# Side work that states how long it holds PSUM, and begins a chain only where the chain fits

## The chip, the cores and the metric

The kernel runs on one core of a Trainium2 chip. The core has a matrix engine (TensorE, PE in the profile; its weight loads are PEld), a vector engine (VectorE, DVE), an activation engine (ScalarE, ACT), a general engine (GpSimd, POOL) and an engine that here only issues DMAs (SyncE, SP). Each engine works through its own queue in order; semaphores make one wait for another. The metric is the device time of one launch in microseconds, lower is better.

## The reference

The input is an image batch of 4 x 64 x 64 pixels with 96 channels. Four layers follow each other, each with a residual sum. Layers 0 and 1 are selective scans over the image; layers 2 and 3 are an attention of linear form and a feed-forward net with values quantized to 8 bits. Cut to the scan layers, whose side work is what changes:

```python
x = x + conv_ref(_gn(x), ...)                  # layers 0 and 1
    xz = x @ in_proj_w.T;  xi, z = split(xz)   # 96 -> 192 + 192
    xc = silu(depthwise_conv3x3(xi) + conv_b)
    xs = four orders of the pixels of xc       # K = 4 directions
    dts, Bs, Cs = split(einsum(xs, x_proj_w))  # per pixel: 6 + 16 + 16
    delta = softplus(dts @ dt_w + dt_b);  A = -exp(A_logs)
    h = exp(delta * A) * h + delta * u * B     # along 4096 pixels, 16 states
    y = sum over states of h * C  + D * xs;  back to image order, summed over K
    y = (y - mean) * rsqrt(var + 1e-5) * ln_w + ln_b
    out = (y * silu(z)) @ out_proj_w.T         # 192 -> 96
t = t + attention(ln(t));  t = t + ffn(ln(t))  # layers 2 and 3
```

`_gn` normalizes groups of three channels over the whole image, so a layer's convolution can begin only when its input's statistics are there.

## The kernel before, in words

**Phases, blocks, tiles.** A phase is one scan layer for one pair of images: phases 0 and 1 are layer 0, phases 2 and 3 layer 1. Two images share the 128 partitions. A phase has 16 blocks (4 directions k by 4 stretches t of 1024 pixels), and a block 48 tiles: 2 groups g of 8 states, 3 channel groups j, 8 states n. A tile is one state's scan over 1024 pixels for 64 channels of two images, 3,072 tiles in all. The main loop (L1046) goes through them by number i; i modulo 48 is called the tile's place in its block.

**What a tile does.** `begin` (two tiles ahead) makes the decay exp(delta A) on ACT in a buffer f, or, for five of 16 states (`POOL_N`), the product with B on POOL, and then the decay goes to the PSUM buffer psB (`decays`). `row` spreads B into psB with PE for the others, `product` multiplies it on DVE. `scan` (L684, DVE) runs the recurrence, `weigh` (L695, POOL) multiplies by C, `gather` sums pairs of tiles into psY with PE. B and C rows come by DMA as copies `brep` and `crep` (L642) on SP's queue, seven to nine tiles ahead.

**The next block's preparation.** `prepare` puts the tasks for the next block (loads, permutation, projections, softplus, copies) at fixed places of the current one. It uses the two PSUM slots called psM, and returns `kept`, the 16 places 17 to 32 (before a block with k = 0) or 13 to 28 (before others), in which psM belongs to it.

**Side work.** Two generators give all other work of the scan layers in pieces; each `yield` ends a piece. `behind(ph)` sets their order: in phase 0 the rest of its own convolution and that of phase 1; in phase ph the tail of phase ph-1, then the convolution of phase ph+1; in phase 3 also the weights of the feed-forward net and the first 12 units of its own tail.

- `conv_pieces`: statistics of the input (16 loads, `bn_stats`, two small matmuls with a psM slot each), then 8 tiles of 512 pixels. A tile has 3 chains j: 9 taps of two matmuls each into the slot px (L289), Silu to xo (L296), two matmuls into the slot pz (L299), Silu to zo (L304), and two stores (L305, L306). `load` fetches the padded input of the next tile. `done` counts finished tiles.
- `tail_pieces`: 16 units of 256 pixels per phase: load yu and zu, transpose into two psM slots (L360) with statistics on ACT, a power on POOL (L372), normalize, transpose back into psM (L387), scale on ACT (L392), gate by z on DVE (L398), the last projection into psM plus the residual xr (L426 to L442), copies and stores. `ready` counts finished units.

**The driver.** In each step of the main loop outside `kept`, `advance` takes one piece (L1090). What a piece yields tells whether it left a psM slot in use: `True` or `MORE` for yes, `False` for no; `MORE` marks a convolution tap, of which a second is taken in the same step when the convolution is behind its goal (`late_by`). Before `kept` begins, the slots must be free, so at its first place all pieces up to the next `False` are taken in one step (L1085 to L1087). Two other loops take pieces without a bound: at place `min(nexts)` until the next block's convolution tiles are finished (L1081 to L1084), and at a phase's change until all are (L1071).

**The last stage.** After the tiles, layers 2 and 3 are put in order by `run`, which keeps a model time for each of its threads. One thread, `remaining`, takes one tail piece at a time; quarters of images 2 and 3 wait for the tail's units. DMAs of all stages are issued by SP in the order of the program.

Of the kernel before, what the change touches and what calls it, by code (L numbers as in the profile page):

```python
# [15 lines left out]
C = 96  # L16
# [18 lines left out]
def kernel(ctx: ExitStack, tc: tile.TileContext, ins, out, layers=(0, 1, 2, 3)):  # L35
# [131 lines left out]
    def mlp_weights():  # L167
# [11 lines left out]
        def quantized(q, src, shape):  # L179
            t = wide(shape, "wq")  # L180
            nc.sync.dma_start(t, src)
            yield False
            yield False
            nc.vector.tensor_copy(q, t, saturate=False)
# [22 lines left out]
    MORE = 2  # L207
# [4 lines left out]
    def conv_pieces(w, xin, xc, zg, done):  # L212
# [9 lines left out]
        yield False  # L222
        yield False
        for i in range(2):
            stats = small([C, NT, 6], "gst")
            for t in range(NT):
                if t:
                    yield False
# [5 lines left out]
            yield False  # L234
            pm = psM([C, 1])
            nc.tensor.matmul(pm, gmat, mv[:, 0:1], start=True, stop=True)
            yield True
# [6 lines left out]
            yield False  # L244
            pv = psM([C, 1])
            nc.tensor.matmul(pv, gmat, dev, start=True, stop=True)
            yield True
# [4 lines left out]
            yield False  # L252
# [23 lines left out]

        done.append(now[0])
        coming = load(0)
        for t in range(NT):
            pads, coming = coming, None  # L280
            yield False
            for i in range(2):
                nc.scalar.activation(pads[i][1], pads[i][1], AF.Identity, bias=norms[i][1], scale=norms[i][0])  # L283
            yield False
            for j in range(J):
                px = psM([128, T])
                for tap in range(9):
# [6 lines left out]
                    yield MORE if tap < 8 else True  # L294
# [3 lines left out]
                for i in range(2):  # L298
# [3 lines left out]
                    )  # L302
                zo = thin([128, T], "zo")
                nc.scalar.activation(zo, pz, AF.Silu)  # L304
                nc.sync.dma_start(xc[:, j, t * T : (t + 1) * T], xo)  # L305
                nc.sync.dma_start(zg[:, j, t * T : (t + 1) * T], zo)  # L306
                if j == J - 1 and t + 1 < NT:
                    coming = load(t + 1)
                if j == J - 1:
                    done[0] += 1  # L310
                yield False

    def tail_pieces(w, units, y, zg, xin, xout, tokens):
# [10 lines left out]
        coming = None  # L324
        for t in units:
            tt = slice(t * U, (t + 1) * U)
            if coming is None:
                while t * U >= flushed(y):
                    yield False
                coming = load(t)  # L330
                yield False
                yield False
# [4 lines left out]
            xr = st([C, 2, U], F32, "xr", 1)  # L337
            for i in range(2):
                nc.sync.dma_start(xr[:, i, :], xin[i][:, tt])
# [17 lines left out]
            for q in range(2):  # L357
# [5 lines left out]
                if q:  # L363
                    statistics(0, pts)
                pts = pt
                yield True
            statistics(1, pts)
            yield False
# [5 lines left out]
            yield False  # L374
            yield False
# [25 lines left out]
            yield False  # L401
            pn0 = back(0)
            normalize(1)
            yield True
            scaled(pn0)
            pn1 = back(1)
            yield True
            scaled(pn1)
            yield True
            gate(0, pn0)  # L410
# [3 lines left out]
            yield True  # L414
            gate(1, pn1)
            yield True
            if tokens:
                xo = thin([128, 2, 2, C], "xn")
                pos = []
                for i in range(2):  # L420
# [8 lines left out]
                    yield True  # L429
                for i in range(2):  # L430
                    nc.scalar.copy(xo[:, i], pos[i][:, :, 0:C])
                    nc.sync.dma_start(xout[i][tt].rearrange("(q p) c -> p q c", p=128), xo[:, i])
                ready[0] = t + 1
            else:
                xo = thin([C, 2, U], "xn")
                pos = []
                for i in range(2):
# [5 lines left out]
                    yield True  # L443
# [768 lines left out]
```

## Time and profile before

| | us |
|---|---|
| median of three runs (11153.49 to 11181.56) | 11167.48 |
| the profiled execution's own time | 11149.85 |
| its span, from the first to the last instruction | 11148.1 |
| first scan L684 starts, last one ends | 134.5, 10545.7 |
| mean granted PE clock | 0.87 |

The profile is of one execution. Busy time of an engine is the sum of its instructions; idle time is given with the instruction that it came before and what ended it, so "<-DVE f L684 296.6" in a row of POOL reads: before such instructions POOL sat idle and a scan on DVE ended 296.6 us of that. A row of the form `L695 POOL TENSOR_TENSOR f<-f,crep 128x1024 f32 ... x3072 | 7158.9, 2354 | ...` gives line, engine, operation, tiles, shape, number, busy time and mean duration in ns. The busy share in 40 equal slices shows where the engines are dense:

```profile
PE   7978888777777779887788878887778877778777
DVE  3898999999999889989999999999999999999846
ACT  3656556554566646665566656665466655555576
POOL 3989999999999889999999999999999999999846
PEclk8989999888888889998888889998888888888877
```

A digit is tenths of a slice of 279 us. POOL and DVE are nearly full from the second slice to the 37th, PE and ACT are not. The first slice and the last two are outside the tiles or nearly.

### The profile page before, as it was taken

How to read it: one execution, taken by the hardware profiler on the slowest of the kernel's cores; microseconds unless marked ns; L12 is line 12 of the kernel's file. 1: busy time of each engine (PE TensorE's matmuls, PEld its weight loads, DVE VectorE, ACT ScalarE, POOL GpSimd, SP SyncE). 2: the span in 40 equal slices, each digit the busy share in tenths (PEclk: the TensorE clock that was granted, in tenths of full speed). 3: DMA queues.
4: the chain of work that ended last, by engine and by line, in shares of the span. 5: the costliest groups of instructions: out<-in, count | busy, mean ns of one | idle time of the engine just before them, and what ended most of it. 6: DMA issues, size and time to landing. Idle time of an engine off the chain costs nothing. (4 is left out here: it accounts for less than half of the span.)

```text
span 11148.1 us, 101994 instructions
## 1 busy us (share of the span) xinstructions
PE 8910.0 (80%) x30112; PEld 2880.5 (26%) x30112; DVE 9926.4 (89%) x6431; ACT 6423.1 (58%) x10575; POOL 10204.6 (92%) x5102
## 2 busy tenths in 40 slices
PE   7978888777777779887788878887778877778777
PEld 2222222111222212221222222222222322222365
DVE  3898999999999889989999999999999999999846
ACT  3656556554566646665566656665466655555576
POOL 3989999999999889999999999999999999999846
PEclk8989999888888889998888889998888888888877
DMA  5679976897578885798666656665556565556410
GB/s 134 158 141 162 141 160 157 145 134 136 149 171 151 140 151 149 157 159 132 138 169 157 157 146 169 164 159 143 149 157 156 155 149 148 143 137 159 122 33 22
DMA packets 1848188, 1604.57 MB, mean 144 GB/s; under 512 B 1412298, under 2 KB 1482892, under 8 KB 1847628
## 3 DMA queue, kind: packets, MB, share of 16 engines
q1 hardware_dynamic: 1847628, 1598.04, 66.1%
q8 instruction: 237, 3.88, 0.2%
q14 instruction: 323, 2.65, 0.1%
HBM read 1008.37 MB, written 186.65 MB: 107 GB/s over the span
## 5 line engine op out<-in xcount | busy, mean ns | idle before, releaser
L695 POOL TENSOR_TENSOR f<-f,crep 128x1024 f32<-128x1024 f32 x3072 | 7158.9, 2354 | 395.9 <-DVE f L684 296.6
L727 PE MATMUL psY<-f,fold 128*64 128x512 f32 x12288 | 3795.1, 698 | 183.4 <-POOL f L695 182.8
L684 DVE TENSOR_TENSOR_SCAN f<-f,state,psB 128x1024 f32<-128x1024 f32 x1584 | 3717.8, 2347 | 206.2 <-ACT f L669 50.1
L669 ACT ACTIVATE f<-delta,L_a 128x1024 f32<-128x1024 f32 x2112 | 2406.5, 1145 | 903.9 <-PE psY L727 829.8
L676 DVE TENSOR_TENSOR psB<-psB,du 128x1024 f32<-128x1024 f32 x2112 | 2558.9, 1212 | 362.9 <-PE psB L662 322.1
L662 PE MATMUL psB<-spB,sel 96*128 96x512 bf16 x4224 | 1387.8, 414 | 1613.5 <-DVE f L684 1599.0
L652 POOL TENSOR_TENSOR f<-du,brep 128x1024 f32<-128x1024 f32 x960 | 2265.7, 2360 | 127.2 <-PE psY L727 29.4
L684 DVE TENSOR_TENSOR_SCAN f<-psB,state,f 128x1024 f32<-128x1024 f32 x720 | 1676.7, 2329 | 76.8 <-POOL f L652 50.3
L727 PEld LDWEIGHTS psY<-f,fold 128*64 128x64 f32 x12288 | 974.9, 154 | 2525.3 <-issue 1806.8
L690 ACT COPY state<-f 128x1 f32<-128x1 f32 x2304 | 429.7, 188 | 2065.8 <-DVE f L684 2056.7
L669 ACT ACTIVATE psB<-delta,L_a 128x1024 f32<-128x1024 f32 x960 | 1070.2, 1115 | 696.0 <-DVE f L684 636.1
L684 DVE TENSOR_TENSOR_SCAN f<-f,psB 128x1024 f32<-128x1024 f32 x528 | 1208.3, 2288 | 57.6 <-ACT f L669 5.9
L662 PEld LDWEIGHTS <-sel 96*128 96x128 bf16 x4224 | 271.3, 99 | 3320.4 <-DVE f L684 2163.7
L289 PE MATMUL psM<-pad,wf 96*64 96x512 f32 x3456 | 901.4, 623 | 36.0 <-ACT pad L283 28.9
L684 DVE TENSOR_TENSOR_SCAN f<-psB,f 128x1024 f32<-128x1024 f32 x240 | 545.6, 2273 | 102.9 <-ACT psB L669 60.0
L718 PE MATMUL psY<-ysum,ident 128*128 128x512 f32 x768 | 554.5, 862 | 98.3 <-ACT ynew L743 86.7
L585 POOL TENSOR_TENSOR xs<-delta,xs 128x1024 f32<-128x1024 f32 x192 | 452.7, 2358 | 95.0 <-ACT delta L582 95.0
L569 PE MATMUL psM<-proj,dtw 12*128 12x512 f32 x768 | 455.2, 686 | 0.0
L543 PE MATMUL psM<-xs,xp 128*76 128x512 f32 x768 | 414.7, 651 | 5.5 <-DMA xs<-xcd 4.2
L718 PE MATMUL psY<-yold,ident 128*128 128x512 f32 (+2 forms) x960 | 370.6, 526 | 42.2 <-ACT ysum L739 26.7
L289 PEld LDWEIGHTS psM<-pad,wf 96*64 96x64 f32 x3456 | 221.4, 138 | 501.0 <-issue 422.6
L743 ACT COPY ynew<-psY 128x1024 f32<-128x1024 f32 (+2 forms) x312 | 242.4, 818 | 171.5 <-PE psY L727 171.5
(149 smaller groups left out, 6644.6 us busy)
## 6 DMA issues: line engine op xcount, KB each, us to landing
crep<-bc SPq DMA_DIRECT2D x2048, 256.0 KB, 4.8
delta<-delta SPq DMA_DIRECT2D x768, 256.0 KB, 4.8
du<-xs SPq DMA_DIRECT2D x768, 256.0 KB, 6.2
brep<-bc SPq DMA_DIRECT2D x640, 256.0 KB, 4.9
yd<-ynew SPq DMA_DIRECT2D x192, 512.0 KB, 7.8
xraw<-xcd SPq DMA_DIRECT2D x144, 512.0 KB, 8.5
yold<-yd SPq DMA_DIRECT2D x144, 512.0 KB, 8.9
xcd<-xo SPq DMA_DIRECT2D x96, 256.0 KB, 3.0
```

The lines of the kernel that those rows point to most:

```text
L289: nc.tensor.matmul(px[64 * i : 64 * i + 64], w["wf"][:, tap, 64 * j : 64 * j + 64], pads[i][0][:, tap // 3 : tap // 3 + rows, tap % 3 : ta ...
L569: nc.tensor.matmul(pds[-1], order[0][1][64:76, j, :], rests[s][64:76], start=True, stop=True)
L585: nc.gpsimd.tensor_mul(xs[j], deltas[j], xs[j])
L652: nc.gpsimd.tensor_mul(f[:, 1:], made[at]["dus"][j][n % 2], reps[at, 0, n])
L662: nc.tensor.matmul(scanned[i][0][:, ss], sel[:, n, :], made[at]["parts"][:, ss], start=True, stop=True)
L669: nc.scalar.activation(out, made[at]["deltas"][j][n % 2], AF.Exp, scale=W[phases[ph][0]]["a"][:, k, j, n // 2 : n // 2 + 1])
L676: nc.vector.tensor_mul(scanned[i][0], scanned[i][0], made[at]["dus"][j][n % 2])
L684: nc.vector.tensor_tensor_scan(f[:, 1:], a, bu, 0.0 if t == 0 else states[at - 1][:, c : c + 1], ALU.mult, ALU.add)
L690: nc.scalar.copy(states[at][:, c : c + 1], f[:, TB : TB + 1])
L695: nc.gpsimd.tensor_mul(f[:, 0:TB], f[:, 1:], reps[at, 1, n])
L718: nc.tensor.matmul(o, of, v, start=(m % banks == 0), stop=False)
L727: nc.tensor.matmul(py[64 * e : 64 * e + 64, ss], fold, two[e][:, ss], start=False, stop=(n == g * GN + GN - 1),)
```

## The change

Each piece now yields three values. `free(ahead)` says that no psM slot is held, and how many pieces the chain that begins next will need. `held(left, more)` says how many pieces are left until the slots are free, and whether a second piece of the same kind may follow in the step. The driver takes a piece outside `kept` only if a chain is under way or the next one's `ahead` fits into the places left before `kept`; inside a chain it takes a second tap when the convolution is late, as before, or when the pieces left are no fewer than the places left.

The pieces themselves are cut anew. In the convolution the last matmuls (pz) end a piece of their own, so that Silu of xo and Silu of zo are in two steps; the store of zo moves to the first tap of the next chain; the next tile's load moves ahead of the last chain; between tiles there is one empty piece fewer. In the tail the first load has four pieces behind it, the residual's load moves from the unit's begin to after the first normalization, both gates are in one piece, and the output's store with `ready` moves into the next unit's first piece (`away`). A tile of the convolution has 34 pieces for 32, a unit of the tail 14 for 13. The three small matmul steps and the weight loads only yield in the new form.

```diff
-    MORE = 2
+    def free(ahead=0):
+        return 0, ahead, False
+
+    def held(left, more=False):
+        return left, 0, more
...
         for t in range(NT):
             pads, coming = coming, None
-            yield False
             for i in range(2):
                 nc.scalar.activation(pads[i][1], pads[i][1], AF.Identity, bias=norms[i][1], scale=norms[i][0])
-            yield False
+            yield free(6)
             for j in range(J):
+                if outs:
+                    outs.pop()()
+                if j == J - 1 and t + 1 < NT:
+                    coming = load(t + 1)
                 px = psM([128, T])
                 for tap in range(9):
...
-                    yield MORE if tap < 8 else True
+                    yield held(10 - tap, tap < 8)
                 xo = thin([128, T], "xo")
                 nc.scalar.activation(xo, px, AF.Silu, bias=w["cb"][:, j, :])
                 pz = psM([128, T])
...
+                yield held(1)
                 zo = thin([128, T], "zo")
                 nc.scalar.activation(zo, pz, AF.Silu)
                 nc.sync.dma_start(xc[:, j, t * T : (t + 1) * T], xo)
-                nc.sync.dma_start(zg[:, j, t * T : (t + 1) * T], zo)
-                if j == J - 1 and t + 1 < NT:
-                    coming = load(t + 1)
-                if j == J - 1:
-                    done[0] += 1
-                yield False
+                outs.append(lambda j=j, t=t, zo=zo: nc.sync.dma_start(zg[:, j, t * T : (t + 1) * T], zo))
+                yield free(6 if j < J - 1 else 0)
+            outs.pop()()
+            done[0] += 1
...
                 coming = load(t)
-                yield False
-                yield False
+                for m in range(4):
+                    yield free(3 if m == 3 else 0)
...
-            xr = st([C, 2, U], F32, "xr", 1)
-            for i in range(2):
-                nc.sync.dma_start(xr[:, i, :], xin[i][:, tt])
...
                 if q:
                     statistics(0, pts)
+                elif outs:
+                    outs.pop()()
                 pts = pt
-                yield True
+                yield held(2 - q)
...
             normalize(0)
-            yield False
+            xr = st([C, 2, U], F32, "xr", 1)
+            for i in range(2):
+                nc.sync.dma_start(xr[:, i, :], xin[i][:, tt])
+            yield free(5)
             pn0 = back(0)
             normalize(1)
-            yield True
+            yield held(4)
             scaled(pn0)
             pn1 = back(1)
-            yield True
+            yield held(3)
             scaled(pn1)
-            yield True
-            gate(0, pn0)
+            yield held(2)
             n = units.index(t) + 1
             if n < len(units) and units[n] * U < flushed(y):
                 coming = load(units[n])
-            yield True
+            yield held(1)
+            gate(0, pn0)
             gate(1, pn1)
-            yield True
+            yield free(3)
...
-                    yield True
+                    yield held(2 - i)
                 for i in range(2):
                     nc.scalar.copy(xo[:, i], pos[i][:, :, 0:C])
-                    nc.sync.dma_start(xout[i][tt].rearrange("(q p) c -> p q c", p=128), xo[:, i])
-                ready[0] = t + 1
+
+                def away(t=t, tt=tt, xo=xo):
+                    for i in range(2):
+                        nc.sync.dma_start(xout[i][tt].rearrange("(q p) c -> p q c", p=128), xo[:, i])
+                    ready[0] = t + 1
...
-            yield False
+            outs.append(away)
+            yield free(3 if coming else 0)
+            if coming is None:
+                outs.pop()()
...
-                        while holds:
+                        while holds[0]:
                             advance()
...
-                if aside is not None and not (plan and place in kept):
+                room = kept[0] - place if plan and place < kept[0] else per
+                if aside is not None and not (plan and place in kept) and (holds[0] or holds[1] <= room):
                     advance()
-                    if holds == MORE and late_by(i, blocks[at][0]):
+                    if holds[2] and (late_by(i, blocks[at][0]) or holds[0] >= room):
                         advance()
```

## The prediction

> **What bounds the kernel now.** I read busy time per engine first, then the costliest groups, then who waits for whom on POOL and DVE, then the stretches and timelines below.
>
> ```profile
> PE 8910.0 (80%) x30112; PEld 2880.5 (26%) x30112; DVE 9926.4 (89%) x6431; ACT 6423.1 (58%) x10575; POOL 10204.6 (92%) x5102
> L695 POOL TENSOR_TENSOR f<-f,crep 128x1024 f32<-128x1024 f32 x3072 | 7158.9, 2354 | 395.9 <-DVE f L684 296.6
> L652 POOL TENSOR_TENSOR f<-du,brep 128x1024 f32<-128x1024 f32 x960 | 2265.7, 2360 | 127.2 <-PE psY L727 29.4
> L585 POOL TENSOR_TENSOR xs<-delta,xs 128x1024 f32<-128x1024 f32 x192 | 452.7, 2358 | 95.0 <-ACT delta L582 95.0
> ```
>
> POOL carries 48 x 2.354 + 15 x 2.36 + 3 x 2.358 = 155 us a block of 48 tiles by these means; successive POOL multiplies overlap a little, and in the timeline a block whose side pieces do nothing (block 58, from 9593.5) takes 153.6 us. The loop runs from the first scan (134.5) to 10,546 us: 10,411 us for 64 blocks against 64 x 153.6 = 9,830. So some 580 us is stall, and POOL's own idle time between those marks adds up to 575. No rearrangement of side work can gain more than that; outside the loop lie 134 us before and 602 after.
>
> ```profile
> 190.80:261.40 70.60, 65.21 (x277) 20.74 (x274) 20.78 (x20) 25.66 (x36) 23.87 (x11) 1.00 0.41 122
> 398.80:427.50 28.70, 26.14 (x100) 7.94 (x98) 17.59 (x14) 16.43 (x23) 21.96 (x10) 0.94 0.64 168
> 568.70:588.10 19.40, 16.71 (x64) 4.75 (x60) 17.89 (x11) 12.02 (x17) 19.40 (x9) 1.00 0.46 130
> 9593.50:9747.10 153.60, 113.70 (x330) 32.35 (x330) 148.46 (x81) 82.34 (x143) 152.56 (x67) 0.87 0.59 146
> ```
>
> These are stretches (start:end, length, then busy PE, PEld, DVE, ACT, POOL, clock, DMA share, GB/s): the forced pieces of blocks 0, 1 and 2, and block 58. In the first, PE is full with convolution while POOL has 23.9 us of work in 70.6: a heap of pieces starves the scan.
>
> **The change, part by part.** The pieces that each step gets can be counted in both programs' own order of instructions; nothing of it is a guess.
>
> (a) *Heaps after block 2.* Before, 22 steps at the start of a closed stretch (place 13 or 17) drain a chain in one go; 20 of them, with 3 to 7 pieces each, lie in blocks 3 to 62. After, one step gives one forced piece. I took the starts of all 3,072 scans L684 from the timeline and, per place, what an interval exceeds the lower quartile of its place. The eight intervals behind the heaps from block 3 on exceed by about 90 us, but equal places without a heap in comparable blocks (blocks 13 and 14 run no pieces at all, and stall 13 and 10 us there on the permuted input) take part of it. Heap by heap what is left is 0 (block 40) to 9 us (block 62): **-57 us**. Bounds -20 (the same PE and ACT work stalls the steps it moves to) and -90.
>
> (b) *Opening.* Blocks 0 to 2 need two convolution tiles each before place 14. Before, 57, 13 and 5 pieces are forced (48+1 and 8; 4+1 and 8; 5), and POOL idles 70.6-23.9 = 46.7, 28.7-22.0 = 6.7 and 0 us: 53 us, 0.71 a piece. After, a tile has 34 pieces for 32 and chains wait for room, so 51, 23 and 24 are forced: 98 x 0.71 = 70, **+16 us**. A chain of 18 taps and its pz takes PE 9.0 us there (7.95 + 1.03 in the timeline), so 23 pieces are two chains and more. Bounds: 0 if the two tiles of lead swallow the new heaps, +36 if the 47 pieces of blocks 1 and 2 cost 0.9 each less the 6.7 paid now.
>
> (c) *First unit of a tail.* Its load now has four empty pieces behind it in place of two.
>
> ```profile
> PE psM L360 <- DMA yu<-yd: 32.4, 3, 12.0
> 5471.07 1.01 POOL L372 TENSOR_TENSOR yrstd<-yvar,mhalf 128x4 f32<-128x4 f32 x1 [7.70 <-ACT yvar L370]
> ```
>
> The first line: PE waited for that load three times, up to 12 us. The second is where it reaches the bound engine: ACT's statistics are late, POOL sits 7.70 us before the small power. The scans show 9.0 and 8.7 us in phases 1 and 2, 0.9 in phase 3. Two more steps are 6.4 us and cover most: **-14 us**, bounds -18 and 0.
>
> (d) *Table loads.* A wait-free step now lies between xo and zo, and a decay (Exp) falls into it.
>
> ```profile
> L669 ACT ACT_TABLE_LOAD x150 | 192.4, 1283 | 5.3 <-DMA delta<-delta 2.7
> L296 ACT ACT_TABLE_LOAD x87 | 111.6, 1283 | 9.8 <-issue 8.2
> 7181.51 1.28 ACT L296 ACT_TABLE_LOAD   x1
> 7182.80 0.69 ACT L296 ACTIVATE xo<-psM,L_cb 128x512 f32<-128x512 f32 x1
> 7183.39 0.59 ACT L304 ACTIVATE zo<-psM 128x512 f32<-128x512 f32 x1
> 7183.99 1.28 ACT L669 ACT_TABLE_LOAD   x1
> ```
>
> Now xo and zo share one load and the decay pays one more. The program of after holds 461 loads for 303: 79 more at the decays, 81 at zo, 2 fewer at xo. 158 x 1.283 = 203 us of ACT, which is 58% busy; decays are begun two tiles (6.4 us) ahead, and that cover hides them. Without it all 203 would show. What the present pair costs is measured: behind the 50 such pairs clear of heaps and permutes, four intervals exceed by 0.53 us in all (median 0.05). I take half of that for each of 81 new pairs: **+22 us**, bounds 0 and 203.
>
> Here a rule speaks against the change. The Trainium skill (ScalarE: Activation LUTs, "What ACT_TABLE_LOAD costs") puts every switch at about 2.66 us, a drain of 1.38 beside the 1.283. The trace agrees on the load and shows no drain: 0.02 us before it, 0.01 after. By the page ACT would get 158 x 2.66 = 420 us.
>
> (e) *Two taps a step.* Steps with two pieces go from 166 to 266; a tap is two matmuls, 0.86 us of PE at the spacing of 0.43 seen at 6095 us. Segments with double taps exceed by 2.7 us on average (22 of them, median 1.45), without by 1.3 (16, median 1.4). Some 18 such segments more: +25 by the means, nothing by the medians; **+5 us**, bounds 0 and 86 (100 x 0.86).
>
> (f) *Output and residual DMAs, both gates in one step.* zg, xout and xr are issued later, past the copies of B and C rows on SP's queue. SP loses its waits for xo (387 us) and for the previous xr (130 + 36), which held up the rows behind them; but POOL waited for all DMAs only some 65 us. The second gate adds 0.55 us to one DVE step and takes it from the next. **0**, bounds -30 and +10.
>
> (g) *The end.* Units get 14 pieces for 13 and start only with room, so the loop finishes 1 unit fewer: -3 us there (some 50 us of excess for 16 units in phase 2), and 132 pieces are left for the last stage in place of 119.
>
> ```profile
> 10550.00:10810.00 260.00, 203.55 (x1405) 178.07 (x1402) 90.27 (x293) 195.02 (x552) 118.21 (x304) 0.76 0.15 43
> 10810.00:11148.00 338.00, 239.44 (x1849) 191.44 (x1848) 204.86 (x523) 226.06 (x492) 233.68 (x441) 0.73 0.08 22
> ```
>
> No engine is full there; ACT leads with 195 of 260 until the last unit's copy. In ACT's order 224.8 us of work (its instructions by their mean durations) stands ahead of that copy before, 232.4 after, and 263 behind it in both. 7.6 x 260/224.8 = **+9 us**. Bounds 0 and 32 (a unit's rhythm there, 252/8).
>
> **Sum:** -57 + 16 - 14 + 22 + 5 + 0 - 3 + 9 = -22 us. The profiled execution took 11,149.85 (span 11,148.1), 17.6 under the median 11,167.48; on the median the forecast is **11,145**. The forecast's own range, half of the bounds of (a), (d) and (e) being needed to leave it, is 11,110 to 11,170.
>
> **The rivals.**
> *More is gained.* The bad spot of a tail today is place 9 of even blocks, 3 to 6 us ten times, some 40 us in all; units of 14 pieces fall differently (two to a block of 28). With 20 of the 40 gone and (d), (e) at 0: -57 + 16 - 14 - 3 + 9 - 20 = -69, 11,098. Against it: final matmuls now stand at places 39 and 40 of nearly every block, the same places modulo eight.
> *Work only moves.* The heaps' PE and ACT work is the same, so (a) gives 20 and the unit at the end costs its whole 32: -20 + 16 - 14 + 22 + 5 - 3 + 32 = +38, 11,205. For it: PE is 80% busy, and the heap of block 2 costs nothing today.
> *Table loads show (slower).* Place: the steps behind xo and zo in phases 0 to 2, where an accumulator decay L669 must come between two scans. If half of the 203 is exposed, -44 + 102 = +58, 11,225. It decides from (44 + 33)/81 = 0.95 us a pair; below 0.54 there is still a gain. Against it: 0.53 is all that the present pair costs.
> *It doesn't do what it says.* True only for the opening, and counted in (b).
>
> **How the numbers follow.** Forecast 0.50, more gained 0.19, work moves 0.16, loads show 0.15. About 0.3%, 33 us, is what a measurement of this kernel can tell from no change (its three runs spread by 28); faster means under 11,134. The forecast gives 0.19 faster and 0.31 same; more gained is all faster; of work moves 0.05 is same and 0.11 slower; of loads 0.02 and 0.13. Faster 0.38, same 0.38, slower 0.24. The range takes in the rivals up to their points: 11,080 to 11,220.
>
> **What would show it.** (a) POOL's wait for L684 (296.6) falls by 40 or more and scans at places 15 to 20 from block 3 run even; (b) three PE-full stretches in the first 600 us, POOL idle some 20 us in the second and third; (c) no wait of PE for yu over 5 us; (d) 461 loads, with DVE's waits for the decays' f and psB (58 + 84) no more than 25 us up; (g) last scan to end 600 to 635 us. The prediction is wrong if the loop's gain is under 10 us, or the end grows by more than 32.

## The result, and the profile after

| | before | after |
|---|---|---|
| median of 4 runs, us (of before's first three: 11167.48) | 11170.94 | 11300.46 |
| profiled span, us | 11148.1 | 11301.0 |
| loop: first scan starts to last scan ends, us | 10,411 | 10,538 |
| last scan to the last instruction, us | 602.4 | 629.5 |
| mean granted PE clock | 0.870 | 0.856 |

The change makes the kernel slower: ratio 1.0121, 95% interval 1.0101 to 1.0140. The loop took 127 us more and the last stage 27 us, in one profiled execution of each kernel. These two lie 153 us apart, the medians 130: before's profiled one is 21 us under its median, so what follows accounts for some 20 us more than the typical loss. The forecast was 11,145 with a range of 11,080 to 11,220, so the time lies outside it.

The first lines below are from the profile of after: busy time per engine, the granted clock in 40 slices, and the two rows of POOL that bound the loop.

```profile
PE 9004.1 (80%) x30112; PEld 2910.9 (26%) x30112; DVE 9943.6 (88%) x6431; ACT 6635.3 (59%) x10733; POOL 10203.7 (90%) x5102
PEclk8989898888888888988888888999888888888877
L718 POOL TENSOR_TENSOR f<-f,crep 128x1024 f32<-128x1024 f32 x3072 | 7165.4, 2356 | 522.9 <-DVE f L707 413.0
L675 POOL TENSOR_TENSOR f<-du,brep 128x1024 f32<-128x1024 f32 x960 | 2266.9, 2361 | 169.5 <-DMA crep<-bc 39.2
```

POOL has the same work (10,203.7 us for 10,204.6) and is idle more: the multiplies by C wait 413.0 us for scans (296.6 before), the multiplies by B 169.5 us in all (127.2). PE has the same 30,112 matmuls and needs 94 us more for them; its granted clock is at nine tenths in fewer slices (7 for 11). Of ACT's 212 us more, 203 are 158 table loads. The waits of after (engine, what it is about to do, what ended the wait: us, times, longest):

```profile
POOL f L718 <- DVE f L707: 413.0, 286, 27.7
DVE psB L699 <- PE psB L685: 405.1, 297, 4.9
POOL yrstd L381 <- ACT yvar L379: 59.2, 12, 13.1
PE psM L367 <- DMA yu<-yd: 9.2, 2, 5.9
```

The last line is the one step that the change was sure of: PE waits 9.2 us for a unit's load, where it was 32.4. But the chain behind POOL has a second link. DVE's products wait 405.1 us for PE (322.1 before), and so PE is late more often. The three stretches of the opening and the two of the end (start:end, length, then busy PE, PEld, DVE, ACT, POOL, clock, DMA share, GB/s) are:

```profile
189.50:260.00 70.50, 62.69 (x253) 19.56 (x249) 29.22 (x24) 27.55 (x42) 32.84 (x15) 0.98 0.49 136
396.00:425.00 29.00, 25.77 (x103) 8.26 (x100) 9.93 (x6) 13.18 (x18) 11.15 (x6) 0.91 0.42 126
573.00:602.00 29.00, 24.94 (x104) 7.70 (x104) 11.51 (x6) 15.44 (x20) 11.53 (x6) 0.94 0.49 149
10671.40:10950.30 278.90, 216.93 (x1441) 187.07 (x1440) 99.56 (x339) 204.03 (x583) 130.42 (x331) 0.76 0.16 46
10950.30:11301.00 350.70, 240.62 (x1836) 191.83 (x1834) 198.78 (x505) 224.48 (x491) 220.98 (x425) 0.72 0.08 22
```

The second and third heap are now of one kind: 29 us, PE full, POOL idle for 17.9 and 17.5. The end takes 14 us more to the last copy of a tail unit (278.9 for 264.8) and 13 behind it (350.7 for 337.6).

To see where the loop's 127 us lie, each interval between the starts of two scans was compared with the quiet interval of its place (the smaller of the two kernels' lower quartiles there), and the excess, called stall below, was put down to the side work that ran with it:

| stall, us | before | after |
|---|---|---|
| opening, blocks 0 to 2 | 101 | 121 |
| beside convolution | 159 | 225 |
| beside tails | 272 | 353 |
| beside the rest or nothing | 187 | 146 |
| sum | 719 | 846 |

How much falls to each of the lower three rows depends on which intervals are given to which piece: with every interval given to the pieces of the four steps before it, the rise is 47 us beside convolution, 48 beside tails and 11 beside the rest. What follows rests on single spots, not on this split.

Finer: in the eight intervals behind each of the 20 heaps from block 3 on, stall fell from 92 to 33 us, as forecast (block 48: 8.1 to 0.2, block 62: 9.7 to 1.2). Behind the last projections of the 55 units that a loop finishes (four intervals, from the step after a unit's first projection on) it rose from 92.7 to 171.7. Under the new rule 15 units project first at place 0 and 15 at place 34, and these pay 4.7 and 3.8 us each. Here is one, the PE timeline of after in block 37 at place 0 (start, us, engine, line, operation, number, and in brackets the idle time before and what ended it). L685 spreads B rows into psB, L455 and L457 are the projection, L750 sums finished tiles into psY:

```profile
6300.90 1.03 PE L685 MATMUL psB<-spB,sel 96*128 96x512 bf16 x2 [4.82 <-DVE f L707]
6301.72 1.06 PE L455 MATMUL psM<-xr,ident 96*96 96x256 f32 x2
6302.71 2.87 PE L457 MATMUL psM<-zu,ow 64*96 64x256 f32 x6
6305.52 2.95 PE L750 MATMUL psY<-f,fold 128*64 128x512 f32 x8
6308.40 0.60 PE L685 MATMUL psB<-spB,sel 96*128 96x512 bf16 x2
6308.84 0.59 PE L455 MATMUL psM<-xr,ident 96*96 96x256 f32 x2
6309.37 1.53 PE L457 MATMUL psM<-zu,ow 64*96 64x256 f32 x6
```

Read the durations of equal groups down the column: L685 takes 1.03 and then 0.60, L455 1.06 and 0.59, L457 2.87 and 1.53. PE has paused for 4.82 us, and for the next 6.7 us it runs at about half its speed. The clock that was granted to it (0.50, then 1.00; third figure from the end) says the same of these stretches:

```profile
6300.90:6307.60 6.70, 6.70 (x16) 2.97 (x18) 5.65 (x3) 1.41 (x3) 4.71 (x3) 0.50 1.07 262
6307.60:6311.00 3.40, 3.40 (x15) 1.49 (x12) 1.85 (x2) 2.46 (x6) 2.02 (x1) 1.00 1.02 266
```

The projection that should take 2 us takes 4, the sum behind it is late, and ACT's timeline of the same microseconds shows the next link:

```profile
6308.54 1.07 ACT L766 COPY ynew<-psY 128x512 f32<-128x512 f32 x2 [5.24 <-PE psY L750]
6309.60 1.13 ACT L692 ACTIVATE psB<-delta,L_a 128x1024 f32<-128x1024 f32 x1
```

ACT waits 5.24 us for psY, and a decay that the scans need (L692) stands behind that copy. In these microseconds DVE was idle 2.38 us and POOL 3.37. POOL's wait ends with a copy of C rows by DMA. Such waits of its products rose from 20.5 us in before to 39.2 in after, and they are 14.5 in the run below that keeps PE busy and leaves the DMAs in their order, so they follow the stall and do not make it.

The Trainium skill (TensorE: Matmul & The Clock Gate, Part 1) describes such a gate: after an idle window of about 3.4 us the array gets half of its clock pulses until it has been busy for about as long. The pause and the two speeds above agree with it; the half clock lasted about twice as long here, and it was met behind shorter pauses too (2.5 us ahead of the projections at place 34). The same page puts the penalty of this ramp under 1% of a typical kernel's span; here the projections' stall is 171.7 of 11,301 us, 1.5%, and its growth is the largest part of what the loop lost.

### The profile page after: what moved, and what is told of

Same layout as the page of the kernel before. It is cut to its first block, busy times and chain, and to the rows that moved or that the text cites. A ratio compares the mean times of both kernels' runs of the same rounds, so it can differ in the third digit from the quotient of the medians.

```text
span 11301.0 us, 102140 instructions
## 1 busy us (share of the span) xinstructions
PE 9004.1 (80%) x30112; PEld 2910.9 (26%) x30112; DVE 9943.6 (88%) x6431; ACT 6635.3 (59%) x10733; POOL 10203.7 (90%) x5102
## 5 line engine op out<-in xcount | busy, mean ns | idle before, releaser
L718 POOL TENSOR_TENSOR f<-f,crep 128x1024 f32<-128x1024 f32 x3072 | 7165.4, 2356 | 522.9 <-DVE f L707 413.0
L750 PE MATMUL psY<-f,fold 128*64 128x512 f32 x12288 | 3771.4, 701 | 161.0 <-POOL f L718 160.3
L692 ACT ACTIVATE f<-delta,L_a 128x1024 f32<-128x1024 f32 x2112 | 2408.6, 1145 | 988.1 <-PE psY L750 897.8
L699 DVE TENSOR_TENSOR psB<-psB,du 128x1024 f32<-128x1024 f32 x2112 | 2558.5, 1211 | 458.9 <-PE psB L685 405.1
L685 PE MATMUL psB<-spB,sel 96*128 96x512 bf16 x4224 | 1406.9, 420 | 1626.0 <-DVE f L707 1595.8
L675 POOL TENSOR_TENSOR f<-du,brep 128x1024 f32<-128x1024 f32 x960 | 2266.9, 2361 | 169.5 <-DMA crep<-bc 39.2
L750 PEld LDWEIGHTS psY<-f,fold 128*64 128x64 f32 x12288 | 952.7, 155 | 2524.2 <-issue 1818.0
L692 ACT ACTIVATE psB<-delta,L_a 128x1024 f32<-128x1024 f32 x960 | 1070.7, 1115 | 625.0 <-DVE f L707 576.8
L685 PEld LDWEIGHTS <-sel 96*128 96x128 bf16 x4224 | 274.5, 99 | 3320.8 <-DVE f L707 2106.4
L300 PE MATMUL psM<-pad,wf 96*64 96x512 f32 x3456 | 872.7, 622 | 7.1 <-ACT pad L290 4.0
L741 PE MATMUL psY<-ysum,ident 128*128 128x512 f32 x768 | 589.5, 912 | 73.3 <-ACT ynew L766 60.2
```

What stands on the lines that cost most here:

```text
L300: nc.tensor.matmul(px[64 * i : 64 * i + 64], w["wf"][:, tap, 64 * j : 64 * j + 64], pads[i][0][:, tap // 3 : tap // 3 + rows, tap % 3 : ta ...
L675: nc.gpsimd.tensor_mul(f[:, 1:], made[at]["dus"][j][n % 2], reps[at, 0, n])
L685: nc.tensor.matmul(scanned[i][0][:, ss], sel[:, n, :], made[at]["parts"][:, ss], start=True, stop=True)
L692: nc.scalar.activation(out, made[at]["deltas"][j][n % 2], AF.Exp, scale=W[phases[ph][0]]["a"][:, k, j, n // 2 : n // 2 + 1])
L699: nc.vector.tensor_mul(scanned[i][0], scanned[i][0], made[at]["dus"][j][n % 2])
L718: nc.gpsimd.tensor_mul(f[:, 0:TB], f[:, 1:], reps[at, 1, n])
```

## The experiments

Four theories stood against each other. *Places*: the new rule puts the last projections where PE has just been idle, so they run at half clock and delay the scans. *Cut*: the new pieces of the tail are themselves dearer. *Loads*: the 158 additional table loads show. *DMA order*: the stores and loads that were moved hold up rows of B and C. Each ratio below is to runs of before taken beside it, with its 95% interval; loop and end are those of the profiled execution.

**Move the projections by two steps.** Two empty pieces after the gates; the first projections then stand at 8, 10, 40 and 42.

```diff
             gate(1, pn1)
+            yield free()
+            yield free()
             yield free(3)
```

> Two empty pieces are put between the gates and the last projection of each tail unit; nothing else is changed. The projections then begin at places 8, 10, 40 and 42 instead of 0, 4, 34 and 38. Places (after 11,300 us; the tail's new cost is that its two last projections stand where PE has paused over 3 us and runs at half clock, 3.1 us of stall a unit against 1.7 before): the loop loses 80 to 150 us, the fold matmuls behind the projections fall from 1.05 to 0.6-0.7 us, the end grows by 15 to 30 (164 pieces left for 132): 11,180 to 11,240. Table loads or the new cut of the pieces as the cause: the loop stays, only the end grows: 11,310 to 11,330.

Measured: 11263.58, ratio 1.0086 (1.0069 to 1.0103); loop 10,497, 41 us less where 80 to 150 were forecast. The projections' stall is 134.6, not 171.7: 0.17 us at place 40, but 4.17 at 42 (18 units), 3.2 at 8 and 1.5 at 10. Place 10 had cost 0.06 in before. So place alone is no price list; what counts is the clock that the projection finds. Of the nine units at place 8, six find 0.50 (the mean over the 3 us from the projection's start) and pay 2.9 to 5.1 us, two find 1.00 and pay 0.01 each. The pause right ahead need not be long for that: at 42, PE's last pause is 1.1 to 1.6 us, with one of 1.9 to 3.4 us some three to seven us ahead of the projection, and the clock is 0.50 to 0.69.

**One table load for xo and zo again.** Silu of xo is moved down to Silu of zo (299 loads).

```diff
-                xo = thin([128, T], "xo")
-                nc.scalar.activation(xo, px, AF.Silu, bias=w["cb"][:, j, :])
                 pz = psM([128, T])
...
                 yield held(1)
+                xo = thin([128, T], "xo")
+                nc.scalar.activation(xo, px, AF.Silu, bias=w["cb"][:, j, :])
                 zo = thin([128, T], "zo")
```

> In the convolution Silu of xo is moved into the step of Silu of zo, so that one table load serves both again (299 loads in the program for 461); every piece stays at its place. Table loads as the main cause (81 pairs of loads, up to 203 us of ACT): 100 us or more come back, 11,200 or below. Places of the tail as the main cause: only the convolution's part comes back, 10 to 35 us: 11,265 to 11,290.

Measured: 11281.49, ratio 1.0098 (1.0081 to 1.0115); loop 10,500, 38 us less than after; the end, 645, is 15 us longer, which was not followed up. The stall beside convolution goes from 225 to 176, 49 us for 81 pairs: 0.6 us each; by the loop as a whole it is 0.5. Groups of ACT's table loads, after first:

```profile
L692 ACT ACT_TABLE_LOAD x229 | 293.8, 1283 | 6.8 <-DMA delta<-delta 2.7
L316 ACT ACT_TABLE_LOAD x81 | 103.9, 1283 | 18.9 <-DMA xcd<-xo 17.4
```

And in this kernel:

```profile
L692 ACT ACT_TABLE_LOAD x148 | 189.9, 1283 | 6.7 <-DMA delta<-delta 2.7 <-PE psY L750 1.5
```

The 81 at zo are gone and 81 of 229 at the decays. The loads do show: some 38 to 49 of the loop's 127 us.

**The old cut of the tail under the new rule.** The generator's pieces as they were in before, each with the counts that the driver wants, and with the residual's load and the output's store where they were; the projections stand at the same places 0, 4, 34 and 38.

```diff
-                for m in range(4):
-                    yield free(3 if m == 3 else 0)
+                yield free()
+                yield free(3)
...
             normalize(0)
-            yield free(5)
+            yield free(7)
             pn0 = back(0)
             normalize(1)
-            yield held(4)
+            yield held(7)
...
-            yield held(2)
+            yield held(5)
+            gate(0, pn0)
...
-            gate(0, pn0)
+            yield held(4)
             gate(1, pn1)
-            yield free(3)
+            yield held(3)
```

> The tail's pieces are cut as before (13 a unit, gates in two pieces, residual loaded at the unit's begin, outputs stored at once), under the new rule, which puts the last projections at the same places 0, 4, 34, 38 as in the changed kernel. Places: the tail's stall stays (3 us a unit), only the end shrinks by 5 to 15: 11,275 to 11,300. The new cut of the pieces as the cause (later DMAs, two gates in one step): 60 to 90 us come back: 11,210 to 11,240.

Measured: 11303.93, ratio 1.0123 (1.0108 to 1.0138); loop 10,539, projections' stall 157. The theory of the cut falls: by itself it changes nothing.

**The new pieces under the old rule.** The driver no longer asks for room, and drains a chain in one step ahead of the closed places, so the forced pieces are back, 113 of them.

```diff
-                if aside is not None and not (plan and place in kept) and (holds[0] or holds[1] <= room):
+                if aside is not None and not (plan and place in kept):
                     advance()
-                    if holds[2] and (late_by(i, blocks[at][0]) or holds[0] >= room):
+                    if holds[2] and late_by(i, blocks[at][0]):
```

> The new pieces under the old driver: a piece in every open step, heaps before the closed places again (113 pieces in them). The projections then stand at eleven different places. Places: the tail's stall falls by 30 to 80 us, the heaps cost some 30 again, the convolution keeps its loads: 11,230 to 11,280. If heaps cost what was predicted of them (57 us) and places nothing: 11,340 to 11,360.

Measured: 11269.62, ratio 1.0092 (1.0077 to 1.0107); loop 10,519. With all the heaps the loop is 19 us shorter than without: what the rule saves at the heaps it gives back, and more, at the projections (some 120 here, at eleven places, 171.7 with the rule).

**Keep PE busy ahead of the projections.** The kernel after, with ten matmuls of a zero matrix in those of the three quiet steps ahead of a unit's projections in which a psY sum is open, 1,270 in all. They add zeros to that sum.

```diff
+            def busy_pe():
...
+                for m in range(10):
+                    nc.tensor.matmul(py[0:64, m % 2 * T : m % 2 * T + T], zero, sel..., start=False, stop=False)
...
             scaled(pn1)
+            busy_pe()
             yield held(2)
```

(The same call stands after the next unit's load and after the second gate.)

> The changed kernel with every piece at its place; in the three quiet steps of a tail unit before the last projections (scale, load, gates) PE gets ten small matmuls of zeros each, which add nothing to psY (1,270 in all, some 270 us of PE at full clock). Half clock (the projections stall the tiles because PE has just paused and runs at half speed): with the pause filled, the fold matmuls behind the projections take 0.6-0.7 us for 1.05 and the 172 us of stall behind the 55 projections fall to 40-90: 11,180 to 11,250. Amount of PE work (two bursts of projections are simply too much for their steps): more matmuls on PE make it no better or worse, 11,300 to 11,360.

Measured: 11216.39, ratio 1.0045 (1.0032 to 1.0059); loop 10,453, end 629.4. More work for PE, 85 us less in the loop: the stall beside tails falls from 353 to 258, that behind the projections from 171.7 to 38.8. PE's timeline of this kernel at the same place of block 37 (the lines of tail and tiles stand 20 further down; L335 is the filler), and the clock granted in these microseconds:

```profile
6275.90 2.32 PE L335 MATMUL psY<-sel,zero 96*64 96x512 bf16 x10
6278.16 0.61 PE L705 MATMUL psB<-spB,sel 96*128 96x512 bf16 x2
6278.60 0.60 PE L475 MATMUL psM<-xr,ident 96*96 96x256 f32 x2
6279.12 1.53 PE L477 MATMUL psM<-zu,ow 64*96 64x256 f32 x6
6280.59 1.94 PE L770 MATMUL psY<-f,fold 128*64 128x512 f32 x8
6275.90:6282.50 6.60, 6.60 (x30) 2.85 (x29) 6.50 (x4) 2.59 (x4) 6.60 (x4) 1.00 1.07 251
```

There is no pause, the first projection takes 1.53 us for 2.87, and the sum behind it 1.94 for 2.95. The whole profile agrees: PE's busy time is 102 us more than in after for 1,270 more matmuls, and POOL waits less:

```profile
PE 9105.9 (81%) x31382; PEld 2989.1 (27%) x31382; DVE 9942.3 (89%) x6432; ACT 6640.3 (59%) x10733; POOL 10202.8 (91%) x5102
POOL f L738 <- DVE f L727: 358.6, 248, 29.4
```

The filler is not free: the projections give back 133 us and the loop only 85, so the other intervals have grown by some 48.

**The control: the same filler too early.** 1,250 zero matmuls in three steps eight to ten steps ahead of the projections (statistics, power, the empty step).

```diff
             statistics(1, pts)
+            busy_pe()
             yield free()
...
             nc.gpsimd.tensor_mul(nb, nmean, rstd)
+            busy_pe()
             yield free()
+            busy_pe()
             yield free()
```

> Control for e5: the same matmuls of zeros (1,250) in the changed kernel, but in three steps of a unit that lie eight to ten steps ahead of its last projections (statistics, power, empty). Half clock just ahead of the projections as the cause: the filler is at the wrong place, the 172 us of stall behind the projections stay above 130: 11,280 to 11,320. If any more work on PE helps wherever it stands (a clock that is higher on the mean): 11,210 to 11,250, as e5.

Measured: 11330.09, ratio 1.0141 (1.0127 to 1.0155); loop 10,569, projections' stall 165.8. One matmul of the sum behind those at place 0 still takes 1.06 us, as in after; with the filler in the right place it takes 0.61. The loop is 31 us longer than after's, and the time lies above both forecasts. Filler is not good in itself. It helps where it keeps the clock up for a burst that others wait for. That settles the theory of places, and turns it into one of the clock.

**Choose the places.** In after, a unit's chain of transposes waits until the step stands at one of five places, so that the projections fall at 10 (24 units) and 41 (24 units).

```diff
             yield free(5)
+            while y is not yd[-1] and now[0] % per not in STARTS:
+                yield free(5)
...
+    STARTS = (5, 36, 39, 45, 46)
```

> In the changed kernel a chain of a tail unit (except the last phase's own tail) waits until its first piece falls on place 5 or 36, which puts the last projections at 10 and 41; pieces and their number are as in the changed kernel (132 left for the end). Places: chains that began at 5 and 36 cost 0.4 to 1.0 us in all other runs, against 4.3 at 43 and more at 29 to 33; the loop falls by 60 to 110 us: 11,190 to 11,240. If it is not the place, 11,290 to 11,310.

Measured: 11226.84, ratio 1.0056 (1.0041 to 1.0072); loop 10,450, projections' stall 88: 0.11 us each at 10, 3.06 at 41. The steps ahead are the same, the clock is not. Here are, for one unit at 10 and one at 41, the last long pause on PE and the clock over the 3 us from the projection's start:

```profile
3170.80 1.03 PE L689 MATMUL psB<-spB,sel 96*128 96x512 bf16 x2 [3.60 <-DVE f L711]
3180.90:3183.90 3.00, 3.00 (x12) 1.55 (x11) 3.00 (x2) 1.47 (x3) 3.00 (x2) 1.00 0.00 0
3286.55 1.03 PE L689 MATMUL psB<-spB,sel 96*128 96x512 bf16 x2 [3.43 <-DVE f L711]
3287.40:3290.40 3.00, 3.00 (x8) 1.72 (x7) 2.90 (x3) 1.45 (x3) 3.00 (x3) 0.50 0.90 277
```

At 10 the pause ended 10 us before the projection, and other matmuls bore the half clock; at 41 it ended 0.8 us before. All 24 units at 10 find the clock at 1.00. At 41, 17 find 0.50 to 0.66 and pay 2.8 to 5.6 us, and seven find 0.97 to 1.00 and pay nothing (at most 0.03). The same reading of each unit in the other traces:

| kernel | units at a clock under 0.7, their stall | the other units, their stall |
|---|---|---|
| before | 16, 63 us | 39, 31 us (23 of it at place 17, in heaps) |
| after | 46, 165 us | 9, 6 us |
| projections two steps later | 27, 125 us | 27, 9 us |
| filler ahead | 4, 12 us | 51, 26 us |
| filler too early | 48, 160 us | 7, 5 us |
| chosen places | 22, 85 us | 33, 3 us |

The length of the last pause alone does not tell the clock: at 41 some units find 0.50 behind a pause of 1.9 to 2.1 us and others 1.00 behind one of 2.7.

**Both repairs.** The places of the last run and the single load.

```diff
+            while y is not yd[-1] and now[0] % per not in STARTS:
+                yield free(5)
...
                 yield held(1)
+                xo = thin([128, T], "xo")
+                nc.scalar.activation(xo, px, AF.Silu, bias=w["cb"][:, j, :])
```

> As e6, with the two Silu of a convolution chain side by side as in e2. If both causes are apart, the gains add: the loop falls by 60 to 110 and by 38 more, 11,150 to 11,210, which is about the kernel before. If they share one cause (the same half clock), less: 11,200 to 11,240.

Measured: 11158.13, ratio 0.9994 (0.9979 to 1.0008); loop 10,409, stall beside convolution 176 as with the load alone. In the profiled loops the two repairs add up, 88 + 38 for 129 us, and the loop is back at before's 10,411. The ratios show more than that, 1.27% together for 0.65% and 0.23% alone; the long end of the run with the single load is part of it, and the profiled executions of these kernels lie up to 15 us from their medians, before's 21. Repairing these two thus takes back what the loop had lost, within that margin; what the opening and the heaps change besides nearly cancels.

**The places, put into before.** Before's pieces and driver, with the same choice of starts and with four empty pieces behind a first load.

```diff
             normalize(0)
             yield False
+            while y is not yd[-1] and now[0] % per not in STARTS:
+                yield False
...
                 coming = load(t)
-                yield False
-                yield False
+                for _ in range(4):
+                    yield False
```

> The kernel before, with its pieces and its driver, but chains of a tail unit begin at places 5 and 36 alone (so that none meets a closed place), and the first unit's load has four empty pieces behind it. Places: the 93 us of stall behind the projections fall to 20-40, heaps of the tail vanish, the loads' wait too: 11,060 to 11,120, ratio 0.990 to 0.996. If places are not what costs, 11,160 to 11,180.

Measured: 11141.8, ratio 0.9980 (0.9966 to 0.9994); loop 10,401, end 607.5. Short of what was hoped: the projections' stall fell only to 73.9 (24 units at 41 pay 2.13 each), and the stall beside convolution rose from 159 to 195, perhaps because tails that wait for their place end later and the convolution behind them catches up with double taps; that was not tried alone.

**Filler alone, put into before.** 1,080 zero matmuls, outside the heaps only.

```diff
             scaled(pn1)
+            busy_pe()
...
             gate(0, pn0)
+            busy_pe()
...
             gate(1, pn1)
+            busy_pe()
```

> The kernel before with e5's filler in the steps ahead of the last projections (not in heaps). Half clock: of its 93 us behind the projections those outside the heaps, some 55, fall to 15-25: 11,110 to 11,140, ratio 0.996 to 0.998. If the clock is no cost before: 11,160 to 11,190.

Measured: 11153.42, ratio 0.9984 (0.9975 to 0.9992); loop 10,408, projections' stall 92.7 to 53.1. The projections give back 40 us and the profiled loop only 3, so here the other intervals eat nearly all of the gain, and the time lies above the forecast. The ten units at place 6 go from 3.86 us each to 0.02; those inside heaps, which got no filler, keep 3.05 (place 13) and 4.17 (place 17).

**Places and filler.** The two last kernels' edits together, 1,350 zero matmuls.

```diff
+            while y is not yd[-1] and now[0] % per not in STARTS:
+                yield False
...
             scaled(pn1)
+            busy_pe()
```

> e8 (chains of the tail at places 5 and 36) with the same filler. Half clock: its 74 us behind the projections, 51 of them at place 41, fall to 20-35: 11,090 to 11,115, ratio 0.993 to 0.996. Otherwise as e8, 11,130 to 11,160.

Measured: 11107.26, ratio 0.9943 (0.9931 to 0.9956). It is faster than both kernels. Loop 10,376, end 604.6; projections' stall 34.3, with 0.27 us each at place 41 for 2.13. From its profile and its waits:

```profile
PE 9047.7 (81%) x31462; PEld 2996.3 (27%) x31462; DVE 9929.2 (89%) x6432; ACT 6433.4 (58%) x10575; POOL 10206.9 (92%) x5102
POOL f L719 <- DVE f L708: 289.5, 198, 29.1
DVE psB L700 <- PE psB L686: 294.2, 254, 6.7
```

DVE's waits for PE are at 294.2 us, against 405.1 in after and 322.1 in before.

**Fewer pieces left for the end.** After, but chains of the last three blocks need no room and the last twelve steps give two pieces, so that 113 pieces are left over in place of 132.

```diff
-                if aside is not None and not (plan and place in kept) and (holds[0] or holds[1] <= room):
+                if aside is not None and not (plan and place in kept) and (holds[0] or holds[1] <= room or at >= 61):
                     advance()
+                if at == 63 and place >= 36 and aside is not None:
+                    advance()
```

> The changed kernel, in which chains of the last three blocks need no room and the last twelve steps give two pieces each, so that 113 pieces are left for the last stage in place of 132; all else is the changed kernel's. If the end follows the tail's rhythm (27 us more for 13 pieces from before to after, 2.1 a piece), it falls from 629 to 585-600 us and the whole to 11,255 to 11,275. If ACT's work decides (0.7 us a piece), the end is 612 to 620 and the whole 11,280 to 11,295.

Measured: 11285.26, ratio 1.0110 (1.0093 to 1.0127). The end takes 603.9, 25.6 less, the loop 5 more. The end lies between its two forecasts. Over most runs the end follows the pieces that are left: 599.6 to 602.4 at 119, 604.6 and 607.5 at 121, 610.8 at 125, 622.8 at 127, 629.4 to 630.7 at 132 in five of six kernels (645 in the one with the single load). That is about 2 us a piece between 119 and 132, but it is no rule: 113 pieces bring no further gain, and the run with two more empty steps, with 144 pieces of work left, takes 629.1. What sets the end stays open.

The DMA order has no run of its own. The two repairs leave nothing for it in the loop.

## Why the prediction was wrong

- **(a) Heaps, -57: right in the number, in part by luck.** 92 to 33 us, -59. But some 41 of the 92 belonged to projections inside heaps (four at 4.5, six at 3.87), which moved elsewhere; the heap as such gave up about 18.
- **(b) Opening, +16: right.** +20, in the form foreseen: a second and third stretch with PE full and POOL idle some 18 us. (A chain has 9 taps of two matmuls; the 18 taps of the forecast are its matmuls. The edit also puts two more empty pieces behind a convolution's first statistics loads and two behind its first load, which the text on the change does not name.)
- **(c) First unit's load, -14: right in kind, smaller.** PE's waits for yu fell nearly as forecast, to none over 5.9 us, but the scans of the first units stalled 3.7 and 7.1 where they had 9.0 and 8.7, about -7.
- **(d) Table loads, +22: mis-sized.** 461 loads as counted; 49 us of stall, 38 of the loop, come back when the pairs are undone, 0.5 to 0.6 a pair where the sum had 0.27. The price of the old pair of loads, 0.53, was the nearer value: the added pair costs as much as the first, and halving it had no row behind it. In ACT's lines at the end of this text at most 0.02 us pass ahead of a load and 0.01 behind it, so the drain of the Trainium skill (ScalarE: Activation LUTs, "What ACT_TABLE_LOAD costs") is not seen here either.
- **(e) Two taps, +5, and (f) DMAs, 0:** little or nothing of the 127 us is left for them once loads and places are repaired. They were not tried alone.
- **(g) The end, +9: mis-sized, +27.** The sum scaled by ACT's work ahead of the last copy. No engine is full there, and the other bound, a unit's rhythm of 32 us, was the nearer one. The reason given is wrong as well: a unit has 14 pieces in both cuts, not 13 before; the text on the change has the same mistake. One unit fewer fits because a chain must find room, which leaves some of the 32 open places of a block empty.
- **The step that failed: that moving the tail's chains costs nothing.** No term of the sum has it. The prediction saw the symptom, ten stalls of 3 to 6 us at one spot of even blocks, took it for a matter of place, and let it appear only as a possible gain of 20 in "more gained", set aside because "final matmuls now stand at places 39 and 40 of nearly every block". They do not: of 55 first projections nine stand at 38, and 15 each at 0 and 34. The runs showed what makes that spot bad: PE pauses ahead of it and then gets half its clock. The new places put 46 units under half clock where 16 had been, and the projections' stall rose by 79 us. Shown are the pauses, the granted clock of each unit, that units at one place pay or do not pay by the clock they find, and that filling the pause takes 133 of 171.7 us away, while the same filler elsewhere takes 6.
- **The rivals.** "Table loads show" had the sign and a part of the cause: at 0.5 to 0.6 us a pair it alone stays under its point of 0.95. "Work only moves" came nearest in words; what moves is the projection, not the heap's load on PE and ACT, and it costs more at the new place than at the old.
- **The range.** Every bound in it was drawn around work that the diff names. It had no bound for how the re-placed matmuls run, though the rows of before held one: 55 units at 0.06 to 4.5 us.

Added up, in us of the loop: projections +79, loads +38 to +49, opening +20, heaps without their projections -18, first units -7, together +112 to +123 of 127. Each is a difference of two profiled executions, so differences of some few us are not more than noise. What stays open is which pauses of PE cost it the clock, since their length alone does not tell.

## What to carry to other kernels

When side work is moved on an engine that is not full, look at what that engine does just before the new place and at the clock that it is granted there: behind PE's pauses of 3 to 5 us in this kernel, and behind some shorter ones, a burst of matmuls took twice as long, and an engine that works in order passes the delay to everybody. Compare the durations of equal groups in a timeline before believing a mean. A schedule that only evens out the number of pieces can lose more than its heaps cost, and an activation that is split from its neighbour pays table loads of its own when a function of another table falls between them.

## What the hardware showed that was not expected

More matmuls made the changed kernel faster. The 1,270 zero matmuls keep PE busy for 300.6 us; PE's busy time rose by only 102, mostly because the others took 157 us less, and the loop became 85 us shorter. And the two losses can follow each other: in after, a table load can itself lengthen PE's pause. ACT's timeline of block 46:

```profile
7800.42 1.28 ACT L316 ACT_TABLE_LOAD   x1
7801.71 0.60 ACT L316 ACTIVATE zo<-psM 128x512 f32<-128x512 f32 x1
7802.20 1.01 ACT L762 COPY ysum<-psY 128x1024 f32<-128x1024 f32 x1
7803.10 0.20 ACT L713 COPY state<-f 128x1 f32<-128x1 f32 x1
7803.32 1.28 ACT L692 ACT_TABLE_LOAD   x1
```

And PE's, of the same microseconds:

```profile
7803.26 3.78 PE L741 MATMUL psY<-yold,ident 128*128 128x512 f32 x4 [4.75 <-ACT ysum L762]
7806.98 3.15 PE L750 MATMUL psY<-f,fold 128*64 128x512 f32 x8
```

The copy of psY stands behind zo's load and Silu; PE waits 4.75 us for it and then runs at half clock (0.50 is granted from 7803.30 to 7807.00, 0.60 in the 3.10 us after): the 8 sums take 3.15 us where the group at full clock above takes 1.94. How much of the 49 us goes this way was not separated.
